# A convolution regrouped by row parity, and a scan layer's hand-written order written anew (one Trainium2 core)

## The chip, the core and the metric

The kernel runs on one core of one Trainium2 chip. The metric is device microseconds of that core. Before the change it takes 26001.39 us, the median of three runs from 25991.08 to 26007.60 us.

## The reference, cut to what matters

The input is 8 images of 128 x 128 positions and 96 channels. Layer 0 (a Fourier filter and a feed-forward net) is untouched by the change. Layer 1 sees the same numbers as 4 images of 32 x 256, and does:

```python
xz = x @ W_in.T;  xc, z = xz[..., :192], xz[..., 192:]
xc = silu(depthwise_conv3x3(xc, conv_w) + conv_b)      # 9 taps a channel
u = stack([xc, xc[reversed]])                          # two directions
dt_r, B, C = split(u @ x_proj);  delta = softplus(dt_r @ dt_proj + b)
# for each direction, channel and state n of 16, along the whole image:
h = exp(delta * A_n) * h + (delta * u) * B_n
y = sum_n(h * C_n);  y = y_forward + y_backward + u * D
out = (y * silu(z)) @ W_out.T                          # then residual, FFN
```

In the code a row of the convolution is 128 positions; a chunk has 8 rows, 1024 positions.

## The kernel before

The trace shows layer 0 for about 4956 us, then the scan layer (`scan_layer`) to the end. Its work goes in **jobs**: batches are taken in four pairs, and for each pair 16 chunks forward (`d == 0`) and then 16 backward (`d == 1`), so 128 jobs. A job has 12 **blocks** (32 channels with 4 states each on the 128 partitions) and a block has 4 **units** `j` (four of the 16 states each), so 48 units. In a block:

- TensorE spreads `delta * u` over the states into the PSUM tile `dub` (L1268, one buffer; two products of 512 columns, each recorded as two matmuls).
- ScalarE makes the decays `da = exp(delta * A)` (L1281), one per unit, in PSUM, two buffers.
- VectorE makes the **injections** `hp = bt * dub` (L1298): one instruction for units 0 and 1 and one for units 2 and 3, 2048 wide. Then it runs the **scan** of each unit over `hp` (L1333).
- GpSimd multiplies each scanned unit by `ct` (L1349, tile `hc`, three buffers), and TensorE sums over the states into `y` (L1358, `total`).
- ScalarE saves the scan's last column (L1342, `keep`).

In a **shared** block ScalarE copies `dub` to SBUF (`fetch`, L1310, tile `dus`), GpSimd does the injection of unit 3 (L1317) and VectorE's second injection is only 1024 wide. `SHARE` names 10 of 12 blocks forward and 4 of 12 backward.

Beside the scans, a forward job does the convolution for the forward job two places later (18 places earlier work for the next pair's first chunks): per job three tiles, each in two halves of nine diagonal products (L1101, tile `pv`), an eviction with bias on ScalarE (L1115), a silu between two table loads (L1126, L1127), and a store to `ud`. Each job also prepares the next one's `delta` and `du` (`prepare_steps`: L1162, L1179, L1190, softplus between two table loads L1193 and L1194, L1201). Backward jobs also gate, project, normalise and run the feed-forward net (`finish_steps`).

The order is written by hand. `plan(at, f)` notes a step with a time in units (48 a job, `UN`), and `emit` records all steps sorted by that time; each engine then works off its own queue strictly in that order. SyncE issues every DMA, in that order too. So a number in `plan` is a place in queues, not a time. In a block that begins at `gb`, the VectorE order before is: injection 0 (`gb`), scan 0, injection 2 (`gb + 1`), scans 1, 2, 3. The other tiles that matter: `hp` has four buffers of two units, `bt` three, `ct` five, `dlb` (the delta broadcast, by DMA L1255) three, `y` one PSUM bank, and `pp` one bank for all small products.

Of the kernel before, what the change touches and what calls it, by code (L numbers as in the profile page):

```python
# [29 lines left out]
TC = 1024  # L30
# [10 lines left out]

def col(ap, p0=None, p1=None):

    v = ap.rearrange("(p o) -> p o", o=1)
    return v if p0 is None else v[p0:p1]
# [8 lines left out]
class Plan:  # L54
# [17 lines left out]
    def emit(self):  # L72
        for _, _, f in sorted(self.steps, key=lambda x: x[:2]):
            f()
# [887 lines left out]
def scan_layer(tc, p, x2d, xcd, zsd, ud, yfd, dld, bcd, out):  # L962
# [11 lines left out]
    with ExitStack() as ctx:  # L974
# [13 lines left out]
        cwt = cp.tile([128, 2, 9], F32, name="cwt")  # L988
        cbt = cp.tile([128, 2], F32, name="cbt")
        for k, parts in enumerate(kinds):  # L990
            for q, c in parts:
                nc.sync.dma_start(cwt[q, k, :], p.conv_w[c, :])
                nc.sync.dma_start(cbt[q, k : k + 1], col(p.conv_b, c.start, c.stop))
        cdiag = cp.tile([128, 2, 9, 128], F32, name="cdiag")
        for k in range(2):
            for j in range(9):
                nc.vector.tensor_scalar(
                    cdiag[:, k, j, :], ident, cwt[:, k, j : j + 1], None, ALU.mult
                )
# [74 lines left out]
        def conv_steps(plan, bp, c, slots):  # L1074
# [3 lines left out]

            def load(t, st):
                def f():  # L1080
                    xin = wk.tile([128, HB + 2, W + 2], F32, tag="xin", name="xin")
                    nc.gpsimd.memset(xin[:, :, 0:1], 0.0)
                    nc.gpsimd.memset(xin[:, :, W + 1 : W + 2], 0.0)
                    for q, b, ch in tile_parts(0, t):
                        nc.sync.dma_start(
                            xin[q, :, 1 : W + 1],
                            xcd[ds(bp * 2 + b, 1), ch, c * HB : c * HB + HB + 2, :].rearrange(
                                "o d h w -> (o d) h w"
                            ),
                        )  # L1090
                    st["xin"] = xin

                return f

            def taps(t, st, i, js):
                def f():
                    if js[0] == 0:
                        st["pv"] = ps1.tile([128, HB // 2, W], F32, tag="pp", name="pv")
                    for j in js:
                        r = i * (HB // 2) + j // 3  # L1100
                        nc.tensor.matmul(  # L1101
                            st["pv"],
                            cdiag[:, kind(t), j, :],
                            st["xin"][:, r : r + HB // 2, j % 3 : j % 3 + W],
                            start=(j == 0),
                            stop=(j == 8),
                        )

                return f

            def evict(t, st, i, hs):
                def f():
                    if i == 0:
                        st["pre"] = w1.tile([128, TC], F32, tag="pre", name="pre")
                    nc.scalar.activation(  # L1115
                        st["pre"][:, hs],
                        st["pv"].rearrange("p h w -> p (h w)"),
                        AF.Identity,
                        bias=cbt[:, kind(t) : kind(t) + 1],
                    )  # L1120

                return f
# [8 lines left out]
            def store(t, st):  # L1131
                def f():
                    nc.sync.dma_start(ud[bp % 2, t, :, c * TC : (c + 1) * TC], st["pre"])

                return f

            for t, begin in enumerate(slots):
                st = {}
                plan(begin[0] - 9, load(t, st))
                for at, (i, hs) in zip(begin, halves()):  # L1140
                    for n, js in enumerate(((0, 1), (2, 3), (4, 5), (6, 7), (8,))):
                        plan(at + n, taps(t, st, i, js))
                    plan(at + 4.4, evict(t, st, i, hs))
                plan(begin[1] + 5, silu(t, st))
                plan(begin[1] + 6.9, store(t, st))

        def prepare_steps(plan, bp, d, c, k, at0):


            k.u, k.du = [None] * 3, [None] * 3  # L1150
# [5 lines left out]
            def project(i, hs):  # L1156
                def f():
# [7 lines left out]
                    k.px = px  # L1165
# [3 lines left out]
            def projected(hs):  # L1169
                nc.scalar.copy(k.bc[:, hs], k.px)  # L1170
# [5 lines left out]
            def delta(t, st, i, hs):  # L1176
                def f():
# [4 lines left out]
                    st["pd"] = pd  # L1182
# [3 lines left out]
            def biased(t, st, i, hs):  # L1186
# [3 lines left out]
                nc.scalar.activation(st["w"][:, hs], st["pd"], AF.Identity, bias=bias)  # L1190
# [12 lines left out]
            for t, at in ((0, 0.4), (1, 3.2), (2, 4.2)):  # L1203
                plan(at0 + at, lambda t=t: load(t))
            for i, hs in halves():
                plan(at0 + 9.2 + 1.3 * i, project(i, hs))
                plan(at0 + 10.2 + 1.1 * i, lambda hs=hs: projected(hs))
            plan(at0 + 12, store_bc)
            for t, at in ((0, PREP[0]), (2, PREP[1]), (1, PREP[2])):
                st = {}  # L1210
                for i, hs in halves():
                    plan(at0 + at["delta"][i], delta(t, st, i, hs))
                    plan(
                        at0 + at["delta"][i] + 0.6,
                        lambda t=t, st=st, i=i, hs=hs: biased(t, st, i, hs),
                    )
                plan(at0 + at["softplus"], lambda st=st: softplus(st))
                plan(at0 + at["mul"], lambda t=t, st=st: mul(t, st))
                plan(at0 + at["store"], lambda t=t, st=st: store(t, st))

        def scan_steps(plan, bp, d, c, k, at0, share):

            bt, ct = {}, {}
# [67 lines left out]
            def inject(blk, j, units):  # L1293
                def f():
                    shared = "dus" in blk and j == 2
# [18 lines left out]
            def inject_shared(blk, units):  # L1314
                def f():
                    hp = blk["hp"] = states_of(blk, 2, units)
                    nc.gpsimd.tensor_tensor(  # L1317
                        hp[:, 1, :], bt[blk["b2"], 2][:, 1, :], blk["dus"], ALU.mult
                    )
# [106 lines left out]
            for m, (b2, t, rr) in enumerate(pairs):  # L1426
# [3 lines left out]
                if m % 3 == 0:  # L1430
                    plan(gm - 12.5, load_b(b2, 0))
                    plan(gm - 3.5, load_b(b2, 2))
                    for j, ahead in enumerate((11.5, 2.5, 1.5, 0.5)):
                        plan(gm - ahead, load_c(b2, j))
                plan(gm - 5, load_pair(pr))
                plan(gm + 2.4, load_z(pr))
                plan(gm + 1.95, open_pair(pr))
                for k2 in range(2):
# [3 lines left out]
                    plan(gb - 7, load_delta(blk))  # L1442
                    plan(gb - 2.5, spread(blk))
                    units = [{} for _ in range(NG)]
                    if 2 * m + k2 in share:
                        plan(gb + 0.1, fetch(blk))
                        plan(gb + 0.5, inject_shared(blk, units))
                    for j, un in enumerate(units):
                        g = gb + j
                        plan(g - 1, decay(blk, j, un))  # L1450
                        plan(g + 1 - 0.05, keep(un))
                        plan(g + 1, read(blk, j, un))
                        plan(g + 2, total(blk, j, un, pr))
                    for at1, f, j in (
                        (0.00, inject, 0),
                        (0.01, scan, 0),
                        (1.00, inject, 2),
# [5 lines left out]
                plan(gm + 9.6, close_pair(pr))  # L1463
                plan(at0 + GATE[m], gate(pr))
                plan(gm + 13.5, store_pair(pr))
            return prs

        def finish_steps(plan, bp, c, prs, i, at0, x2_at, at):
# [181 lines left out]
        PREP = tuple(  # L1650
            {"delta": (a0, a1), "softplus": e, "store": e + 1.9, "mul": m}
            for a0, a1, e, m in (
                (12.2, 13.2, 16.2, 19.3),
                (24.2, 25.2, 28.2, 31.3),
                (37.2, 38.2, 41.2, 45.3),
            )
        )

        SLOTS = ((3.2, 16.2), (26.2, 31.1), (39.1, 43.6))

        def conv_slots(bp, n):
# [3 lines left out]
            if bp > 0 and n < 2:  # L1665
                ahead = [18] * 3
            elif bp > 0 and n == 2:
                ahead = [18, 18, 2]
                slots = ((3.2, 14.3), (19.0, 30.1), SLOTS[2])
# [4 lines left out]
        SHARE = ((0, 1, 2, 3, 4, 6, 7, 8, 9, 11), (1, 4, 7, 10))  # L1674
        GATE = (9.9, 17.9, 25.9, 37.3, 41.9, 50.5)

        FINISH = (
            (
                (14.5, (28.2, 29.6, 30.2, 31.2, 32.2, 40.2, 42.2, 42.2, 44.2, 44.8, 45.4, 46.2,
                46.4, 47.2, 46.6, 47.2, 47.4, 48.2, 47.6, 48.2, 48.4, 48.6, 49.2, 50.2, 52.2,  # L1680
                53.2)),
                (27.5, (40.2, 43.2, 43.8, 44.4, 45.2, 46.2, 49.2, 50.2, 51.2, 51.8, 54.2, 54.8,
                55.2, 55.4, 55.2, 56.2, 56.4, 56.6, 63.2, 63.8, 64.2, 65.2, 70.6, 71.4, 73.2,
                76.2)),
            ),
            (
                (43.5, (52.2, 54.2, 54.8, 55.2, 56.3, 57.2, 60.2, 61.2, 62.2, 62.8, 66.2, 66.8,
                68.2, 69.2, 68.2, 69.2, 69.4, 70.2, 69.6, 70.2, 71.2, 71.4, 74.2, 75.2, 77.2,
                78.2)),
                (55.5, (64.2, 65.6, 66.2, 68.2, 68.2, 76.2, 77.2, 77.2, 78.2, 78.8, 79.4, 80.2,  # L1690
                80.4, 80.6, 80.6, 81.2, 81.4, 82.2, 81.6, 82.2, 82.4, 83.2, 83.8, 84.6, 85.2,
                89.4)),
            ),
        )
        with tc.manual_schedule():
# [4 lines left out]
            for bp in range(B // 2):  # L1700
# [4 lines left out]
                for n, (d, c) in enumerate(jobs):  # L1705
# [3 lines left out]
                    share = SHARE[0 if d == 0 and (bp == 0 or n > 0) else 1]  # L1709
# [10 lines left out]
            plan.emit()  # L1720
# [126 lines left out]
```

## Time and profile before

| | us |
|---|---|
| median of three runs | 26001.39 |
| the profiled execution | 25993.76 |
| its span, first to last instruction | 25992.0 |
| busy in the span: PE / DVE / ACT / POOL | 22274.3 / 24026.8 / 17774.3 / 21599.5 |
| DMA, share of the 16 engines | 42.3% |

The engines are PE (TensorE), DVE (VectorE), ACT (ScalarE), POOL (GpSimd), SP (SyncE); PEld is the weight load. A line of the group view gives source line, engine, operation, what it writes and reads, its shape and count, and then busy time, mean of one in ns, and idle time before it. The view of waits says who waited for whom: total us, times, longest. The view of stretches gives, for a window, each engine's busy us with its instruction count, then the granted TensorE clock as a share, the DMA share and GB/s. In the time line a bracket tells how long the engine sat idle before the instruction and what released it. SPq is SyncE's DMA queue.

### The profile page before, as it was taken

How to read it: one execution, taken by the hardware profiler on the slowest of the kernel's cores; microseconds unless marked ns; L12 is line 12 of the kernel's file. 1: busy time of each engine (PE TensorE's matmuls, PEld its weight loads, DVE VectorE, ACT ScalarE, POOL GpSimd, SP SyncE). 2: the span in 40 equal slices, each digit the busy share in tenths (PEclk: the TensorE clock that was granted, in tenths of full speed). 3: DMA queues.
4: the chain of work that ended last, by engine and by line, in shares of the span. 5: the costliest groups of instructions: out<-in, count | busy, mean ns of one | idle time of the engine just before them, and what ended most of it. 6: DMA issues, size and time to landing. Idle time of an engine off the chain costs nothing.

```text
span 25992.0 us, 271847 instructions
## 1 busy us (share of the span) xinstructions
PE 22274.3 (86%) x85072; PEld 8926.1 (34%) x85072; DVE 24026.8 (92%) x18135; ACT 17774.3 (68%) x31518; POOL 21599.5 (83%) x13561
## 2 busy tenths in 40 slices
PE   8999999888997777888977778888777788887777
PEld 7777777522222222222222222222222222222222
DVE  7888888699999999999999999999999999999998
ACT  6887777566667777666677776666777766657776
POOL 5666666488889999888899998888999988889998
PEclk9999999999998888999988889999888899988888
DMA  3333333344444444444444444444444444444443
GB/s 89 95 94 91 92 89 88 110 152 150 151 152 142 142 142 140 152 152 152 153 142 141 141 140 152 152 152 153 142 141 141 141 151 153 153 144 140 141 142 117
DMA packets 1887419, 3513.54 MB, mean 135 GB/s; under 512 B 564702, under 2 KB 999510, under 8 KB 1885946
## 3 DMA queue, kind: packets, MB, share of 16 engines
q1 hardware_dynamic: 1885972, 3496.15, 42.3%
q8 instruction: 676, 11.08, 0.2%
q14 instruction: 771, 6.32, 0.1%
HBM read 2739.33 MB, written 756.17 MB: 134 GB/s over the span
## 4 chain that ended last, share of the span: by engine, by line
DVE 31%; PE 21%; issue 10%; ACT 10%; POOL 9%; DMA 0%; DVEq 0%; POOLq 0%; SPq 0%; ACTq 0%
DVE hp L1333 19%; DVE hp L1298 12%; PE pv L1101 7%; PE y L1358 6%; POOL hc L1349 6%; PE dub L1268 4%; ACT da L1281 2%; PE y L1400 1%; ACT L1194 1%; ACT L1193 1%; ACT dus L1310 1%; PE pd L1179 1%; PE px L1162 1%; ACT w L1193 1%; POOL hp L1317 1%
## 5 line engine op out<-in xcount | busy, mean ns | idle before, releaser
L1349 POOL TENSOR_TENSOR hc<-hp,ct 128x1024 f32<-128x1024 f32 x6144 | 14376.0, 2359 | 1280.2 <-DVE hp L1333 1035.2
L1333 DVE TENSOR_TENSOR_SCAN hp<-da,h,hp 128x1024 f32<-128x1024 f32 x6144 | 14169.7, 2338 | 662.6 <-ACT da L1281 494.6
L1358 PE MATMUL y<-hc,sely 128*32 128x512 f32 x24576 | 7157.9, 671 | 2284.0 <-POOL hc L1349 2270.9
L1281 ACT ACTIVATE da<-dlb,at 128x1024 f32<-128x1024 f32 x6144 | 6847.6, 1115 | 0.3 <-ACT h L1342 0.3
L1298 DVE TENSOR_TENSOR hp<-bt,dub 128x2048 f32<-128x2048 f32 (+1 forms) x3072 | 6015.8, 1958 | 430.1 <-ACT dus L1310 273.2
L1268 PE MATMUL dub<-du,selx 128*128 128x512 f32 x6144 | 3484.5, 695 | 485.7 <-DVE hp L1298 485.3
L1101 PE MATMUL pv<-xin,cdiag 128*128 128x512 f32 x6912 | 3511.9, 627 | 75.7 <-ACT pre L1115 54.9
L1342 ACT COPY h<-hp 128x1 f32<-128x1 f32 x6144 | 1152.2, 188 | 3296.7 <-DVE hp L1333 3280.3
L1358 PEld LDWEIGHTS y<-hc,sely 128*32 128x32 f32 x24576 | 964.5, 113 | 6824.9 <-POOL hc L1349 4973.6
L1317 POOL TENSOR_TENSOR hp<-bt,dus 128x1024 f32<-128x1024 f32 x878 | 2075.0, 2363 | 788.8 <-ACT dus L1310 781.3
L1268 PEld LDWEIGHTS dub<-du,selx 128*128 128x128 f32 x6144 | 1224.6, 215 | 2581.6 <-issue 1355.4
L1101 PEld LDWEIGHTS pv<-xin,cdiag 128*128 128x128 f32 x6912 | 1181.3, 192 | 2462.3 <-issue 2061.5
L1115 ACT ACTIVATE pre<-pv,cbt 128x512 f32<-128x512 f32 x384 | 263.9, 687 | 1589.5 <-PE pv L1101 1447.7
L1310 ACT COPY dus<-dub 128x1024 f32<-128x1024 f32 x878 | 887.5, 1011 | 471.8 <-DVE hp L1298 471.7
L110 POOL TENSOR_SCALAR ln_v<-ln_v 128x4 f32<-128x4 f32 x768 | 199.6, 260 | 1125.5 <-DVE ln_v L106 1105.4
L1179 PE MATMUL pd<-bc,dtw 12*128 12x512 f32 x1536 | 977.4, 719 | 9.9 <-ACT w L1190 7.5
L1201 POOL TENSOR_TENSOR du<-w,u 128x1024 f32<-128x1024 f32 x384 | 906.6, 2361 | 42.5 <-ACT w L1193 42.5
L111 POOL TENSOR_TENSOR ln_r<-ln_v,mhalf 128x4 f32<-128x4 f32 x768 | 888.4, 1157 | 64.0
L790 PE MATMUL ring<-xnt,win 96*128 96x512 f32 x1536 | 801.2, 630 | 70.1 <-ACT xnt L784 69.0
L1162 PE MATMUL px<-u,xpw 128*76 128x512 f32 x1536 | 756.4, 630 | 2.2 <-ACT bc L1170 1.2
L1582 ACT CAST ff_h<-ph 128x512 f16<-128x512 f32 x768 | 442.1, 576 | 449.0 <-PE ph L1569 449.0
L1190 ACT ACTIVATE w<-pd,dtb 128x512 f32<-128x512 f32 x768 | 523.7, 682 | 298.8 <-PE pd L1179 263.3
(191 smaller groups left out, 31103.0 us busy)
## 6 DMA issues: line engine op xcount, KB each, us to landing
dlb<-dld SPq DMA_DIRECT2D x1536, 512.0 KB, 4.1
bt<-bcd SPq DMA_DIRECT2D x1024, 512.0 KB, 5.3
ct<-bcd SPq DMA_DIRECT2D x1024, 512.0 KB, 3.9
u<-ud SPq DMA_DIRECT2D x384, 512.0 KB, 5.5
dld<-w SPq DMA_DIRECT2D x384, 512.0 KB, 2.9
ud<-pre SPq DMA_DIRECT2D x192, 512.0 KB, 4.3
yf<-ud SPq DMA_DIRECT2D x768, 128.0 KB, 3.8
yfd<-yo SPq DMA_DIRECT2D x384, 256.0 KB, 6.1
```

What stands on the lines that cost most here:

```text
L1101: nc.tensor.matmul(st["pv"], cdiag[:, kind(t), j, :], st["xin"][:, r : r + HB // 2, j % 3 : j % 3 + W], start=(j == 0), stop=(j == 8),)
L1162: nc.tensor.matmul(px, xpw[:, d, t, :], k.u[t][:, hs], start=(t == 0), stop=(t == 2))
L1179: nc.tensor.matmul(pd, dtw[4 * NST : NX, d, t, :], k.bc[4 * NST : NX, hs], start=True, stop=True)
L1268: nc.tensor.matmul(blk["du"][:, hs], selx[:, blk["r"], :], k.du[blk["t"]][:, hs], start=True, stop=True,)
L1281: nc.scalar.activation(un["da"], blk["dl"], AF.Exp, scale=at[:, d, blk["kb"], j : j + 1])
L1298: nc.vector.tensor_tensor(hp[:, 0:n, :], bt[blk["b2"], j][:, 0:n, :], blk["du"].rearrange("p (o t) -> p o t", o=1).to_broadcast([128, n, TC]),
L1310: nc.scalar.copy(blk["dus"], blk["du"])
L1317: nc.gpsimd.tensor_tensor(hp[:, 1, :], bt[blk["b2"], 2][:, 1, :], blk["dus"], ALU.mult)
L1333: nc.vector.tensor_tensor_scan(h, da, h, un["init"], op0=ALU.mult, op1=ALU.add)
L1342: nc.scalar.copy(un["init"], un["h"][:, last : last + 1])
L1349: nc.gpsimd.tensor_tensor(un["hc"], un["h"], ct[blk["b2"], j], ALU.mult)
L1358: nc.tensor.matmul(y[q, :], sely, un["hc"][:, hs], start=False, stop=(j == NG - 1),)
```

## The change

Three things change in the scan layer, and nothing in layer 0.

**Six products for nine.** A convolution tile holds 64 channels twice: partitions 0 to 63 the even rows, 64 to 127 the odd rows. A product's 128 x 128 weight then carries two taps (the diagonal, and one 64 x 64 corner that reaches the other parity), and six products over four row pairs cover the nine taps. The input comes by four DMAs a tile (before: one or two), the result leaves by four (before: one). The weights take 36 VectorE instructions to build (before: 18) and 12 small loads (before: 6).

**Order of a block.** Every offset of `plan` is now taken from a table `PL`. The VectorE order becomes, forward: scan 2 of the block before, injection 0, its scan 3, injection 2, scans 0, 1, 2. Backward: injection 0, scan 3 of the block before, scan 0, injection 2, scans 1, 2. `fetch` stands ahead of injection 0 and right behind the decay of the block before's unit 3; `keep`, `read` and `total` move, as do the loads, stores, softplus, silu and finishing steps.

**Shares.** 0 is no share, 1 as before, 2 gives GpSimd both units 2 and 3 in one 2048-wide instruction, and VectorE none. Forward jobs: six blocks with 1, two with 2 (10 units as before). Backward jobs, and the first forward job of pairs 1 to 3: seven blocks with 1 (before: four).

```diff
+PL = {'share': ((1, 1, 2, 1, 1, 2, 1, 0, 0, 0, 0, 1), (1, 1, 1, 1, 1, 0, 1, 0, 1, 0, 0, 0),
+           (1, 1, 1, 1, 1, 0, 1, 0, 1, 0, 0, 0)),
+ 'dir': ({
...
+          'ld': -4.15,
+          'spread': -2.82,
+          'inj': [-1.385, -0.77],
...
+          'fetch': -1.63,
+          'ishare': -0.89,
+          'close': 10.26,
+          'decay': [-0.7, -0.82, -1.3, -0.75],
+          'keep': [3.4, 2.72, 2.48, 1.42],
+          'read': [1.95, 1.64, 1.05, 2.84],
+          'total': [3.54, 3.32, 3.17, 3.07],
...
+         {
...
+          'spread': -3.01,
+          'inj': [-1.285, 0.83],
...
+          'fetch': -1.81,
+          'ishare': 0.55,
+          'close': 10.14,
+          'decay': [-1.74, -1.18, -1.83, -1.44],
+          'keep': [5.11, 1.54, 1.17, 0.5],
+          'read': [2.39, 1.7, 1.89, 1.68],
+          'total': [3.46, 2.84, 2.51, 2.83],
...
+ 'slots': ((2.59, 14.73, 20.81, 25.93, -0.67), (25.35, 29.44, 33.54, 41.16, 23.49),
+           (39.92, 44.71, 51.05, 53.43, 34.75)),
+ 'tapd': 1.33,
+ 'cev': 3.19,
...
-        for k in range(2):
-            for j in range(9):
+        for n in range(3):
+            for j in range(6):
+                tap = j if j < 3 else j + 3
                 nc.vector.tensor_scalar(
-                    cdiag[:, k, j, :], ident, cwt[:, k, j : j + 1], None, ALU.mult
+                    cdiag[:, n, j, :], ident, cwt[:, n, tap : tap + 1], None, ALU.mult
+                )
+                r, o = (1, 0) if j < 3 else (0, 1)
+                q = slice(64 * r, 64 * r + 64)
+                nc.vector.tensor_scalar(
+                    cdiag[q, n, j, 64 * o : 64 * o + 64],
...
-                    plan(gb - 7, load_delta(blk))
-                    plan(gb - 2.5, spread(blk))
+                    blk["share"] = share[2 * m + k2]
+                    plan(gb + V["ld"], load_delta(blk))
+                    plan(gb + V["spread"], spread(blk))
                     units = [{} for _ in range(NG)]
-                    if 2 * m + k2 in share:
-                        plan(gb + 0.1, fetch(blk))
-                        plan(gb + 0.5, inject_shared(blk, units))
+                    if blk["share"]:
+                        plan(gb + V["fetch"], fetch(blk))
+                        plan(gb + V["ishare"], inject_shared(blk, units))
                     for j, un in enumerate(units):
                         g = gb + j
-                        plan(g - 1, decay(blk, j, un))
-                        plan(g + 1 - 0.05, keep(un))
-                        plan(g + 1, read(blk, j, un))
-                        plan(g + 2, total(blk, j, un, pr))
+                        plan(g + V["decay"][j], decay(blk, j, un))
+                        plan(g + V["keep"][j], keep(un))
+                        plan(g + V["read"][j], read(blk, j, un))
+                        plan(g + V["total"][j], total(blk, j, un, pr))
                     for at1, f, j in (
-                        (0.00, inject, 0),
+                        (V["inj"][0], inject, 0),
                         (0.01, scan, 0),
-                        (1.00, inject, 2),
+                        (V["inj"][1], inject, 2),
                         (1.01, scan, 1),
                         (2.00, scan, 2),
                         (3.00, scan, 3),
                     ):
                         plan(gb + at1, f(blk, j, units))
```

## The prediction

> **What bounds the kernel now.** I read the view of stretches first, cut at job starts (a job is 72 VectorE scans and injections in the time line): ten forward jobs, twelve backward jobs, and the last forward job, which has no convolution beside it.
>
> ```profile
> 5763.00:7401.40 1638.40, 1471.23 (x3844) 408.81 (x3840) 1517.80 (x721) 1002.86 (x1440) 1423.75 (x671) 0.95 0.47 152
> 8052.60:9998.00 1945.40, 1522.37 (x4896) 469.56 (x4896) 1892.49 (x866) 1413.79 (x2629) 1782.52 (x1021) 0.85 0.42 141
> 23193.60:23346.80 153.20, 111.39 (x276) 26.15 (x276) 150.93 (x74) 86.70 (x129) 141.69 (x62) 0.83 0.42 139
> ```
>
> After the length come PE, PEld, DVE, ACT, POOL and the granted clock. A forward job takes 163.8 us with VectorE busy 151.8; a backward job 162.1, VectorE busy 157.7. VectorE bounds both, but forward it stands still 12 us a job. GpSimd is next: 142.4 us a forward job, 148.5 a backward one. The job without convolution takes 153.2 with the same VectorE work: the convolution costs a forward job some 10 us without one instruction on VectorE.
>
> How, the view of waits of the same windows shows: three lines of VectorE forward, one of ScalarE forward, then VectorE backward.
>
> ```profile
> DVE hp L1333 <- ACT da L1281: 51.3, 60, 1.6
> DVE hp L1298 <- ACT dus L1310: 46.2, 30, 2.3
> DVE hp L1298 <- PE dub L1268: 11.3, 10, 1.3
> ...
> ACT pre L1115 <- PE pv L1101: 224.9, 50, 6.9
> ```
>
> ```profile
> DVE hp L1333 <- ACT da L1281: 36.2, 54, 1.1
> ```
>
> Forward, VectorE waits 5.1 us a job for decays, 4.6 for `dus` and 1.1 for `dub`, while ScalarE stands 22.5 us a job at the head of its queue for the convolution's product. The time line joins the two: the eviction waits 5.17 us, everything behind it in ScalarE's queue is late, and the injection starts 2.30 late, the moment `dus` is done.
>
> ```profile
> 6051.26 0.69 ACT L1115 ACTIVATE pre<-pv,cbt 128x512 f32<-128x512 f32 x1 [5.17 <-PE pv L1101]
> ...
> 6052.98 1.01 ACT L1310 COPY dus<-dub 128x1024 f32<-128x1024 f32 x1
> ...
> 6054.02 1.22 DVE L1298 TENSOR_TENSOR hp<-bt,dub 128x1024 f32<-128x1024 f32 x1 [2.30 <-ACT dus L1310]
> ```
>
> Prices I take from start to start, in a stretch of VectorE's time line without waits:
>
> ```profile
> 8052.60 2.26 DVE L1298 TENSOR_TENSOR hp<-bt,dub 128x2048 f32<-128x2048 f32 x1
> 8054.97 2.35 DVE L1333 TENSOR_TENSOR_SCAN hp<-da,h,hp 128x1024 f32<-128x1024 f32 x1
> 8057.24 2.26 DVE L1298 TENSOR_TENSOR hp<-bt,dub 128x2048 f32<-128x2048 f32 x1
> 8059.41 6.83 DVE L1333 TENSOR_TENSOR_SCAN hp<-da,h,hp 128x1024 f32<-128x1024 f32 x3
> ...
> 8070.79 1.20 DVE L1298 TENSOR_TENSOR hp<-bt,dub 128x1024 f32<-128x1024 f32 x1
> 8071.90 6.83 DVE L1333 TENSOR_TENSOR_SCAN hp<-da,h,hp 128x1024 f32<-128x1024 f32 x3
> ```
>
> A wide injection costs 2.37 (8052.60 to 8054.97) when the next instruction scans what it wrote, 2.17 (8057.24 to 8059.41) when it does not; a narrow one 1.11; a scan 2.25 to 2.27, I take 2.26. The sums stand up: forward 12 x 2.37 + 2 x 2.17 + 10 x 1.11 + 48 x 2.26 = 152.4, plus waits of 10.9, is 163.3 of 163.8; backward 12 x 2.37 + 8 x 2.17 + 4 x 1.11 + 108.5 = 158.7, plus 3.1, is 161.8 of 162.1.
>
> **The change, part by part.**
>
> Order. Injection 0 is now followed by the neighbour's scan 3, so all are priced 2.17: 12 x 0.20 = 2.4 us less a job, both ways.
>
> Shares. Forward VectorE has 12 + 4 wide and 6 narrow injections: 16 x 2.17 + 6 x 1.11 + 108.5 = 149.9. Backward 17 wide and 7 narrow: 153.2. GpSimd keeps 10 units forward, so 142.4 stays under 149.9. Backward it takes three more; four `hc` in a row take 9.30, so 2.33 each: 148.5 + 7.0 = 155.5, above VectorE's 153.2. Backward the bound moves to GpSimd, and 155.5 is the floor.
>
> Six for nine. The products cost 0.43 us a record at full clock (18 records in 7.96 us): 36 records fewer, 15.5 us of TensorE a forward job. None of that is on VectorE's path; it pays only through ScalarE, whose eviction waits less. Its place moves too: the eviction stands 0.53 units behind the last products (before 0.4), and the sums `y`, on which TensorE waits for GpSimd at its queue's head, stand 3.1 to 3.5 units behind their unit (before 2), so the products are less held up. Bounds: nothing gained (10.9 us of waits stay), or all (0.8, the wait of the job without convolution).
>
> The new wait. `fetch` now precedes injection 0, and both read `dub`; the copy is recorded first, so injection 0 waits for it in 8 blocks forward, 7 backward. It stands behind the decay of unit 3, which needs scan 1 over. From there: 1.11 for the decay, 1.01 for the copy and an estimated 0.1 for starts (the injection above starts 0.03 after its copy's end), 2.2 in all, beside scan 2 of 2.26. It just fits. In blocks 1, 3, 5 and 11 forward the copy of `y` (0.58) stands between: 0.5 late, 2 us a job. Behind the waiting injection stand scan 3 and all VectorE work. Softplus and silu with their loads (2 x 1.28 + 1.06 = 3.6 us) now stand mostly behind `fetch`, beside injection 0, scan 3 and injection 2 (5.5 us), so I give them nothing. With 1 us of other delays, forward waits are 3.1 a job, 153.0 in all; bounds 150.5 and 158. Backward VectorE waits 3.1 now behind the feed-forward's ScalarE work; on GpSimd's 155.5 I put 2.5 for the two engines' uneven steps: 158.0; bounds 155.5 and 162.3, where half of GpSimd's present idle time (162.1 - 148.5 = 13.6) remains.
>
> The spread (`dub`) follows injection 2 and precedes `fetch`. At full clock it took 1.96, at a low clock 3.78:
>
> ```profile
> 6000.48 1.96 PE L1268 MATMUL dub<-du,selx 128*128 128x512 f32 x4 [0.94 <-DVE hp L1298]
> ...
> 6013.96 3.78 PE L1268 MATMUL dub<-du,selx 128*128 128x512 f32 x4
> ```
>
> From injection 2 to the copy's turn there are scans 0 and 1 and a decay, 2 x 2.26 + 1.2 = 5.7 us forward, one scan less backward, 3.5. Forward it is hidden either way; backward at full clock only, and at the low one 0.3 late, hidden by GpSimd. Less work on TensorE makes the low clock likelier: the job without convolution had 0.83 against 0.95, and yet waited least. The Trainium skill, "TensorE: Matmul & The Clock Gate", Part 1, speaks against the change here: after an idle window of about 3.4 us the array's clock falls to half. By that rule with every spread on the path, 12 x 1.8 = 22 us a job would be lost; by the row of the job at 0.83, nothing.
>
> DMAs. A forward job issues 17 more (8 inputs, 9 stores), at 0.33 to 0.61 each under 10 us of SyncE's queue, beside about 60 issues. The load of a block's delta falls from 7 units ahead of its block to 4.15 and 3.25; its first decay stands 0.7 and 1.74 ahead, so 3.45 units (11 us) are left forward and 1.5 (5 us) backward, for a landing of 4.1 (median of `dlb`). That is thin backward only if SyncE issues no earlier than the step's place. It does issue earlier: in the view of its waits the longest line is this load waiting for a buffer to come free.
>
> ```profile
> SPq L1255 <- ACT da L1281: 4090.6, 617, 13.0
> ```
>
> I put the DMAs at nothing, with 1 us a job as the other end. `keep` (0.19) moves from ahead of a decay to behind it: up to 0.2 less between a scan's end and the next decay, counted at nothing.
>
> Before the first scan (4956 to 5110) TensorE does twelve nine-product groups at 8.0 us; at 5.3 that is 32 less, 4 more for six small loads: -28. The 57 us after the last scan stay, plus or minus 6.
>
> **Sum.** 62 forward jobs with convolution: 62 x (153.0 - 163.8) = -670. Two without, 154.4 to 151: -7. Backward 64 x (158.0 - 162.1) = -262. Start -28. Together -967; 25993.8 - 967 = 25027 for an execution like the profiled one; the median of the runs stands 7.6 above it: **25034 us**. All lower bounds give 64 x 149.9 and 64 x 155.5 in place of 10457 and 10368, the scans' own total: about 24,690.
>
> **The rivals.**
>
> - GpSimd's saturation (0.17): backward at 162.3, nothing gained, the rest as forecast: 25,310. For it: 155.5 of 158 leaves no slack and `hp` has four buffers. Against: GpSimd behind by a unit or two never starves.
> - The waits stay (0.12): ScalarE's evictions were not the cause, or others take their place. Forward gains its 2.5 us alone, 161.3: 25,540. Against it stands the job of 153.2.
> - Slower (0.06): `dus` is late ahead of injection 0 everywhere. Its present wait is 1.54 when it comes (46.2/30); at all 15 blocks of a forward and a backward job that is 23 us, against 163.8 + 162.1 - 149.9 - 155.5 = 20.5 gained: 26,160. It decides from 1.4 us a block.
> - The floors are reached (0.05): 24,690.
>
> **How the numbers follow.** The forecast has 0.60, its own range 24,740 to 25,300. With GpSimd's rival and most of the second, 24,740 to 25,480 holds 8 in 10. A measurement of this kernel tells about 0.2%, 52 us. Faster by more: the forecast, the floors and the first two rivals without a small remainder, 0.92; within it 0.02; slower 0.06.
>
> **What would show it.** Right: forward jobs near 153 with "pre <- pv" waits under 10 us a job; VectorE's waits for `dus` moved to the wide injection; GpSimd busy 155 of 158 backward; the clock forward below 0.95. Wrong: VectorE waiting over 1.4 us a block for `dus`, GpSimd waiting for `y` or for scans backward, or waits for a DMA on VectorE or ScalarE.

## The result, and the profile after

The changed kernel takes 26051.34 us, the median of 13 runs (26038.47 to 26066.16), beside 25992.88 for the kernel before (13 runs, 25982.32 to 26007.60). The ratio is 1.0022, with a 95% interval of 1.0014 to 1.0031: 0.2% slower, where 25034 us and a range of 24740 to 25480 were predicted. The profiled execution took 26050.59 us, its span 26048.8.

The view of stretches of the kernel after, ten forward jobs and twelve backward ones (length, then PE, PEld, DVE, ACT, POOL with counts, clock, DMA share, GB/s):

```profile
5765.80:7388.80 1623.00, 1338.01 (x3480) 362.25 (x3480) 1501.96 (x701) 984.04 (x1421) 1417.31 (x648) 0.90 0.50 153
8040.10:10009.10 1969.00, 1476.90 (x4896) 483.03 (x4896) 1843.68 (x866) 1442.78 (x2664) 1863.75 (x1057) 0.88 0.42 140
```

A forward job takes 162.3 us (163.8 before; 153.0 forecast), a backward job 164.1 (162.1; 158.0 forecast). Yet VectorE is busy 150.2 and 153.6 us a job, and GpSimd 155.3 backward: the three floors were forecast at 149.9, 153.2 and 155.5. So the work shrank as foretold, and waiting ate it: VectorE now stands still 12.1 us of a forward job and 10.5 of a backward one.

The view of waits in the same two windows, VectorE's main lines and two of ScalarE forward, then VectorE's backward (total us, times, longest):

```profile
DVE hp L1405 <- ACT dus L1417: 109.1, 50, 3.6
DVE hp L1405 <- issue: 11.1, 8, 1.4
...
ACT yo L1522 <- PE y L1473: 47.1, 28, 2.6
ACT pre L1208 <- PE pv L1193: 24.7, 22, 2.1
```

```profile
DVE hp L1405 <- ACT dus L1417: 91.9, 46, 4.9
DVE hp L1405 <- POOL ff_y L1734: 15.1, 10, 1.5
```

Of three kinds of wait forward one is left, and at 12.1 us a job it is larger than the three were together (10.9). ScalarE's wait for the convolution's product fell from 22.5 to 2.5 us a job, and VectorE's wait for decays has nearly gone (12.6 us in the whole scan layer, 492.6 before). But injection 0 waits for the copy `dus`, by the view 10.9 us a job forward and 7.7 backward. The lines that name `issue` or GpSimd in front of injection 0 are the copy too: in every shared block where it is late, it starts 0.03 to 0.10 us after the copy's end (in one case 0.44). Where nothing waits, injection 0 starts 2.24 us after the scan ahead of it. Against that, and as the mean of the ten forward jobs, it is late by 0 / 0.45 / 0 / 3.65 / 3.13 / 1.56 / 2.53 us in blocks 0 to 6, by 1.28 in block 11, and by 0 in the unshared blocks 7 to 10: 12.6 in all.

Why, the time line of ScalarE shows at block 4 of a forward job (start, duration, what; the bracket is idle time before it), and VectorE's beside it:

```profile
11692.85 1.12 ACT L1386 ACTIVATE da<-dlb,at 128x1024 f32<-128x1024 f32 x1 [1.57 <-DVE hp L1448]
11693.91 0.67 ACT L1294 ACTIVATE w<-pd,dtb 128x512 f32<-128x512 f32 x1
11694.59 1.28 ACT L1297 ACT_TABLE_LOAD   x1
11695.89 1.06 ACT L1297 ACTIVATE w<-w 128x1024 f32<-128x1024 f32 x1
11696.96 1.28 ACT L1298 ACT_TABLE_LOAD   x1
11698.26 1.12 ACT L1386 ACTIVATE da<-dlb,at 128x1024 f32<-128x1024 f32 x1
11699.31 1.00 ACT L1417 COPY dus<-dub 128x1024 f32<-128x1024 f32 x1
```

```profile
11690.48 6.82 DVE L1448 TENSOR_TENSOR_SCAN hp<-da,h,hp 128x1024 f32<-128x1024 f32 x3
11700.35 2.29 DVE L1405 TENSOR_TENSOR hp<-bt,dub 128x2048 f32<-128x2048 f32 x1 [3.05 <-ACT dus L1417]
```

Scan 1 is over at 11690.48 + 2 x 2.26 = 11695.0, and decay 3 could start then. It starts at 11698.26, because softplus and its two table loads stand ahead of it in the queue. The copy follows the decay, and the injection starts 0.04 after the copy's end. In block 6 it is silu with its loads; in blocks 1, 3, 5 and 11 the copy of `y` or an eviction, with what each waits for itself.

Block 9 is the control. There, too, silu and its loads stand ahead of decay 3, but the block has no copy, and injection 0 starts without a wait (end of the burst on ScalarE, then VectorE):

```profile
6043.48 1.28 ACT L1220 ACT_TABLE_LOAD   x1
6044.78 1.12 ACT L1386 ACTIVATE da<-dlb,at 128x1024 f32<-128x1024 f32 x1
```

```profile
6037.61 6.82 DVE L1448 TENSOR_TENSOR_SCAN hp<-da,h,hp 128x1024 f32<-128x1024 f32 x3
6044.35 2.26 DVE L1405 TENSOR_TENSOR hp<-bt,dub 128x2048 f32<-128x2048 f32 x1
```

In the run e4 below, where blocks 7 and 9 are shared, injection 0 is late by 5.90 and 3.01 us in them.

### The profile page after: what moved, and what is told of

The parts are those of the page before. It is cut to its first block, busy times and chain, and to the rows that moved or that the text cites. A ratio compares the mean times of both kernels' runs of the same rounds, so it can differ in the third digit from the quotient of the medians.

```text
span 26048.8 us, 268368 instructions
## 1 busy us (share of the span) xinstructions
PE 21191.9 (81%) x82768; PEld 8705.7 (33%) x82768; DVE 23661.7 (91%) x18031; ACT 17822.4 (68%) x31597; POOL 22017.7 (85%) x13640
## 4 chain that ended last, share of the span: by engine, by line
DVE 36%; issue 18%; PE 12%; POOL 9%; ACT 7%; DMA 1%; SPq 0%; POOLq 0%; DVEq 0%; ACTq 0%
DVE hp L1448 19%; DVE hp L1405 17%; POOL hc L1464 7%; PE dub L1373 4%; PE y L1473 3%; ACT da L1386 2%; ACT dus L1417 2%; PE po L1608 1%; PE pv L1193 1%; ACT L1298 1%; POOL du L1305 0%; PE y L1515 0%; POOL hp L1432 0%; ACT yo L1522 0%; PE px L1266 0%
## 5 line engine op out<-in xcount | busy, mean ns | idle before, releaser
L1448 DVE TENSOR_TENSOR_SCAN hp<-da,h,hp 128x1024 f32<-128x1024 f32 x6144 | 14067.3, 2332 | 12.6 <-ACT da L1386 12.6
L1473 PE MATMUL y<-hc,sely 128*32 128x512 f32 x24576 | 6794.9, 658 | 1022.8 <-POOL hc L1464 1013.4
L1405 DVE TENSOR_TENSOR hp<-bt,dub 128x2048 f32<-128x2048 f32 (+1 forms) x2950 | 5797.1, 1965 | 1502.7 <-ACT dus L1417 1176.9
L1373 PE MATMUL dub<-du,selx 128*128 128x512 f32 x6144 | 3832.0, 756 | 1661.6 <-DVE hp L1405 1327.1
L1193 PE MATMUL pv<-xin,cdiag 128*128 128x512 f32 x4608 | 2332.1, 630 | 152.9 <-ACT pre L1208 93.6
L1457 ACT COPY h<-hp 128x1 f32<-128x1 f32 x6144 | 944.3, 185 | 1042.1 <-DVE hp L1448 1037.4
L1193 PEld LDWEIGHTS pv<-xin,cdiag 128*128 128x128 f32 x4608 | 852.6, 199 | 1675.4 <-issue 1444.2
L1515 PE MATMUL y<-yf,ddiag 128*128 128x512 f32 x768 | 532.1, 781 | 484.5 <-ACT yo L1522 484.5
L1522 ACT COPY yo<-y 128x512 f32<-128x512 f32 x768 | 446.0, 581 | 631.4 <-PE y L1473 631.2
L1608 PE MATMUL po<-wo,yo 128*128 128x194 f32 x3072 | 622.5, 353 | 195.0 <-POOL yo L1529 195.0
```

The costliest lines, as they stand in the source:

```text
L1193: nc.tensor.matmul(st["pv", i], cdiag[:, groups(t)[i][1] // 64, j, :], st["xin"][:, i, r : r + HB // 2, j % 3 : j % 3 + W], start=(j == 0) ...
L1373: nc.tensor.matmul(blk["du"][:, hs], selx[:, blk["r"], :], k.du[blk["t"]][:, hs], start=True, stop=True,)
L1405: nc.vector.tensor_tensor(hp[:, 0:n, :], bt[blk["b2"], j][:, 0:n, :], blk["du"].rearrange("p (o t) -> p o t", o=1).to_broadcast([128, n, TC]),
L1448: nc.vector.tensor_tensor_scan(h, da, h, un["init"], op0=ALU.mult, op1=ALU.add)
L1457: nc.scalar.copy(un["init"], un["h"][:, last : last + 1])
L1473: nc.tensor.matmul(y[q, :], sely, un["hc"][:, hs], start=False, stop=(j == NG - 1),)
```

## The experiments

All times are medians, and each ratio is to the kernel before, run beside it on the same chip, with its 95% interval. In the short diffs the first place of a kind is the forward one, the second the backward one. My theory after the result: the copy ahead of injection 0 makes VectorE wait for whatever ScalarE has in its queue. The rivals: the low clock makes the spreads late; GpSimd is the bound backward; the six products themselves cost something. Four of the twelve expected times held (e2, e8, e9, e12); e3 came out faster than its range, and the other seven slower.

**e1, the copy ahead of decay 3.**

```diff
-          'fetch': -1.63,
+          'fetch': -2.8,
...
-          'fetch': -1.81,
+          'fetch': -3.0,
```

> The changed kernel with the copy of dub (fetch) moved up in ScalarE's queue, from behind the decay of the block before's unit 3 to ahead of it (forward -1.63 to -2.8, backward -1.81 to -3.0); nothing else. Theory A (ScalarE's queue): injection 0 waits for the copy only because decay 3, copies of y, evictions, biases and table loads stand ahead of it; the waits fall from about 12 us a forward and 10 us a backward job to under 4, forward jobs near 153, backward near 157: 25,050 us, at most 25,300. Theory B (TensorE's spread ends too late, at the low clock): dub is no earlier, so the waits stay, 25,950 or more.

25832.39 us, 0.9939 [0.9924, 0.9954]. VectorE's waits in the whole scan layer:

```profile
DVE hp L1448 <- ACT da L1386: 598.0, 365, 3.2
DVE hp L1405 <- ACT dus L1417: 258.5, 181, 3.8
```

The waits for `dus` fell from 1165.5 to 258.5, but scans now wait 598.0 for decays that stand behind the copy. A forward job falls to 158.2, a backward one rises to 165.2. The chain was the right one; that it would end there was wrong.

**e2, no shares.** Without a share there is no copy.

```diff
+PL = {'share': ((0,) * 12, (0,) * 12, (0,) * 12),
```

> The changed kernel with no shared block: no copy of dub, VectorE does all injections 2048 wide. Theory A: no wait ahead of injection 0 is left; 24 x 2.17 + 48 x 2.26 = 160.6 us of VectorE a job, about 161 with small waits, 128 jobs: 25,780 us (25,700 to 25,900), so faster than the changed kernel although VectorE has 957 units more to inject. Theory B: the spread is late for unshared blocks as well, 10 us of waits a job stay, 171 a job: 27,000.

25707.61 us, 0.9889 [0.9874, 0.9904]. These are all of VectorE's waits in the scan layer:

```profile
DVE hp L1404 <- PE dub L1372: 15.8, 17, 1.5
DVE hp L1447 <- ACT da L1385: 2.1, 4, 0.6
```

VectorE has 24 wide injections a job here, 24 x 2.17 + 108.5 = 160.6 us, and jobs take 160.4 and 160.6: nothing is waited for at clocks of 0.89 and 0.87. That speaks against the clock rival; the kernel's own trace settles it, in the paragraph on the clock below. The 957 in the expectation counts shared blocks; VectorE gets back 61 x 10 + 67 x 7 = 1079 units. In this order, taking work from VectorE through these shares cost more than the shares were worth.

**e3, the six products alone**, in the order and shares of before. The eviction keeps its place in the order, so it now stands 2.4 units behind the last of three groups of products.

```diff
-for n, js in enumerate(((0, 1), (2, 3), (4, 5), (6, 7), (8,))):
+for n, js in enumerate(((0, 1), (2, 3), (4, 5))):
```

> The kernel before with six products in place of nine, all places in the queues and all shares as before. Theory A: ScalarE's waits for the convolution's product fall from 22.5 us a forward job to about 10, and VectorE's waits from 10.9 to about 5: forward jobs 158, backward unchanged, start 28 less: 25,600 us (25,450 to 25,800). Rival (the evictions' wait was no cause, or more DMAs cost what is gained): forward jobs 163 to 164, 25,950 or more.

25398.51 us, 0.977 [0.9754, 0.9786]. The forward jobs, and the same two waits as above:

```profile
5729.80:7266.40 1536.60, 1315.75 (x3480) 356.85 (x3480) 1512.78 (x721) 1009.07 (x1441) 1421.58 (x671) 0.93 0.53 162
```

```profile
DVE hp L1360 <- ACT da L1308: 11.1, 41, 1.6
...
ACT pre L1132 <- PE pv L1117: 1.5, 4, 0.4
```

A forward job takes 153.7 us with VectorE busy 151.3; backward nothing changes. This is under the expected range: VectorE's waits fell from 10.9 to 1.1 us a job, where 5 was expected. The products are worth 598 us by themselves; what of it is fewer products and what the eviction's greater distance from them, no run tells apart.

**e4, the new order with the old shares.**

```diff
-PL = {'share': ((1, 1, 2, 1, 1, 2, 1, 0, 0, 0, 0, 1), (1, 1, 1, 1, 1, 0, 1, 0, 1, 0, 0, 0),
+PL = {'share': ((1, 1, 1, 1, 1, 0, 1, 1, 1, 1, 0, 1), (0, 1, 0, 0, 1, 0, 0, 1, 0, 0, 1, 0),
```

> The changed kernel with the shares of the kernel before (ten of twelve forward, four of twelve backward). Theory A: the wait goes with shared blocks that have ScalarE work ahead of the copy. Forward 150.0 of VectorE's own work plus 12 to 15 of waits, about 164; backward 156.3 plus about 5, about 161.5: 26,000 us (25,900 to 26,100). Theory B: backward 156.3 plus 10, 166: 26,300.

26215.65 us, 1.0085 [1.007, 1.01]; forward 167.3 with VectorE idle for 16.8 (13.1 of it noted as waiting for `dus`), backward 162.4. With e3 the three parts follow, added one after the other: six products 25398.51 - 25996.64 (the kernel before, beside e3) = -598, new order 26215.65 - 25398.51 = +817, new shares 26051.34 - 26215.65 = -164.

**e5, the copy behind injection 0.**

```diff
-          'fetch': -1.63,
+          'fetch': -1.3,
...
-          'fetch': -1.81,
+          'fetch': -1.2,
```

> The changed kernel with the copy of dub recorded just behind injection 0 (forward -1.63 to -1.3, backward -1.81 to -1.2) in place of ahead of it; nothing else. Theory A (the copy is recorded ahead of injection 0, and both read dub, so injection 0 inherits every delay of ScalarE's queue): injection 0 no longer waits for ScalarE; the copy has scan 3 of the block before to hide under. Forward 150 plus about 2, backward 156 to 158 with GpSimd near 155: 25,000 us (24,850 to 25,200). Rival (ScalarE has too little time in shared blocks wherever the copy stands): the waits reappear before injection 2 and before scans, 7 us or more a job in both directions, 25,700 or more.

25661.88 us, 0.987 [0.9855, 0.9884]; 160.2 us a job both ways, no better than without shares (e2). VectorE's main waits in the scan layer, and one of ScalarE's:

```profile
DVE hp L1448 <- ACT da L1386: 668.8, 338, 3.9
DVE hp L1405 <- PE dub L1373: 294.2, 190, 3.6
...
ACT dus L1417 <- DVE hp L1405: 895.7, 466, 3.6
```

No injection 0 waits for `dus` any more, but now the copy waits for injection 0, at the head of ScalarE's queue; a burst of softplus or silu then comes late, and the next decay behind it (2.56 us in block 1, 3.09 in block 11). As in e1, the lateness moved to the scans, and the time is close to the rival's 25,700.

**e6, six products and seven shares backward, old order.**

```diff
-        SHARE = ((0, 1, 2, 3, 4, 6, 7, 8, 9, 11), (1, 4, 7, 10))
+        SHARE = ((0, 1, 2, 3, 4, 6, 7, 8, 9, 11), (0, 1, 3, 4, 6, 7, 10))
```

> The kernel before with six products and with seven shared blocks backward (0, 1, 3, 4, 6, 7, 10) in place of four; all places in the queues as before. Theory: VectorE backward loses 3 x 1.06 = 3.2 us a job, GpSimd gains 7.0 to 155.5: backward 162.1 to 159.5, forward 153.7: 25,230 us (25,150 to 25,400). Rival (GpSimd near its limit gives the gain back): 25,400 or more.

25473.09 us, 0.9797 [0.9781, 0.9814]. A backward job rises from 162.1 to 163.9 though VectorE's work falls to 154.7: waits for decays of 5.8 and for `dus` of 2.0 a job. These seven shares backward do not pay in the old order either.

**e7, VectorE's new order alone**: the two injections at their new places, the copy just behind injection 0 (not ahead of it, as in the changed kernel) and GpSimd's shared injection moved along; all else as in e3.

```diff
-                        (0.00, inject, 0),
+                        ((-1.385, -1.285)[d], inject, 0),
...
-                        (1.00, inject, 2),
+                        ((-0.77, 0.83)[d], inject, 2),
```

> The kernel before with six products and VectorE's new order (injection 0 ahead of the neighbour's scan 3, injection 2 at its new place), the copy of dub right behind injection 0, all shares and all other places as before. Theory: injection 0 at 2.17 in place of 2.37, 12 x 0.2 = 2.4 us less a job both ways; forward 151.5, backward 160: 25,110 us (25,000 to 25,300). Rival (the new order itself breaks the cover of decays and spreads): slower than the 25,400 of six products alone.

26908.42 us, 1.0352 [1.0336, 1.0367]: 1800 us above the theory's number. In ten forward jobs, VectorE's first wait and one of TensorE's:

```profile
PE y L1385 <- POOL hc L1376: 331.2, 143, 5.0
...
DVE hp L1325 <- PE dub L1295: 184.9, 77, 6.2
```

Injection 0 moved up by 1.4 units and the spread that feeds it did not. The spread stands behind sums `y` that wait for GpSimd at the head of TensorE's queue, so injection 0 waits 18.5 us a job for `dub`. An order is a set: one engine's part of it costs 1500 us against e3.

**e8, shares only where the copy comes in time.**

```diff
+PL = {'share': ((1, 1, 2, 0, 0, 2, 0, 0, 0, 0, 0, 0), (0, 0, 1, 0, 1, 0, 0, 0, 0, 0, 0, 0),
```

> The changed kernel with shares only where its trace shows the copy of dub in time or nearly (forward blocks 0 and 1 with 1, blocks 2 and 5 with 2; backward blocks 2 and 4); nothing else. Theory A: VectorE gets 6 injections back forward (1.06 each, 149.9 to 154.1 with the two-wide ones unchanged) and 5 backward (153.2 to 158.5), and the waits of the blocks taken out go (forward 10.7 of 12.6, backward 9.9 of 10.9): 156 forward, 159.5 backward, 25,370 us (25,250 to 25,500). Rival (lateness of ScalarE only moves on to decays): forward 162 or more, 25,700.

25494.9 us, 0.9812 [0.9795, 0.9828]: 157.0 forward, 160.5 backward, with 38.8 us of waiting for `dus` left in the whole scan layer. Four shared blocks forward and two backward, in place of eight and seven, gain 26051.34 - 25494.9 = 556 us.

**e9, the old forward order and the new backward one without shares**, six products. The forward half of `PL` and the convolution's places are those of before, and so are the shares of forward jobs.

```diff
+PL = {'share': ((1, 1, 1, 1, 1, 0, 1, 1, 1, 1, 0, 1), (0,) * 12, (0, 1, 0, 0, 1, 0, 0, 1, 0, 0, 1, 0)),
...
+          'inj': [0.0, 1.0],
...
+          'fetch': 0.1,
```

> Six products; forward jobs with every place and share of the kernel before, backward jobs with the changed kernel's places and no share. Theory: forward as in the run with six products alone, 153.7; backward as in the run without shares, 160.6, against 162.1: 25,290 us (25,200 to 25,380), the fastest so far. Rival (the two orders disturb each other at the 7 changes of direction, or the finishing steps' places need the shares): 25,400 or more.

25354.75 us, 0.9756 [0.9742, 0.9771]: 153.5 and 160.4 a job.

**e10, the copy of `y` behind the copy of `dub`.**

```diff
-          'close': 10.26,
+          'close': 10.45,
...
-          'close': 10.14,
+          'close': 10.25,
```

> The changed kernel with the copy of y moved from just ahead of the copy of dub to just behind it (forward 10.26 to 10.45, backward 10.14 to 10.25); nothing else. Theory A: in the blocks where it stood between, forward 1, 3, 5 and 11 and backward 1 and 3, the wait before injection 0 falls by the copy and by its own wait for TensorE: about 5 us a forward job (of 12.6) and 4 a backward job (of 10.9): 25,480 us (25,350 to 25,750). Theory B (the spread is late) or a queue that is late anyway: 26,000.

25815.56 us, 0.9935 [0.992, 0.995]; forward 159.1. Blocks 1, 5 and 11 no longer wait and block 3 is late by 0.53 in place of 3.65, but block 2 by 1.08 in place of 0 and block 4 by 4.22 in place of 3.13.

**e11, also the first tile's softplus, silu and second half of the convolution behind it** (and one bias), and no shares backward.

```diff
-          'prep': [[10.01, 12.9, 13.91, 20.94, 14.79],
+          'prep': [[10.1, 12.9, 14.45, 20.94, 14.79],
...
- 'slots': ((2.59, 14.73, 20.81, 25.93, -0.67),
+ 'slots': ((2.59, 15.25, 22.45, 25.93, -0.67),
```

> As the run with the copy of y behind, and forward the three other steps that stand ahead of a copy of dub moved behind it (softplus of the first tile 13.91 to 14.45, its first bias by 0.09, the convolution's first tile: second half 14.73 to 15.25, silu 20.81 to 22.45); backward no shares. Theory A: forward all waits before injection 0 go, 152 to 153; backward 160.6 as in the run without shares: 25,180 us (25,080 to 25,400). Rival (ScalarE's steps now make the decays late): forward 157 or more, 25,500.

25593.14 us, 0.9849 [0.9834, 0.9864]; forward 159.0, no better than e10. VectorE waits 2.9 us a job for decays, 2.9 for `dus`, 1.9 for GpSimd's injections and 1.1 for `dub`: the lateness moved to other steps.

**e12, the best of both halves**: e9 with five shared blocks backward, and there the copy behind injection 0.

```diff
-PL = {'share': ((1, 1, 1, 1, 1, 0, 1, 1, 1, 1, 0, 1), (0,) * 12,
+PL = {'share': ((1, 1, 1, 1, 1, 0, 1, 1, 1, 1, 0, 1), (1, 0, 0, 1, 1, 0, 1, 0, 1, 0, 0, 0),
...
-          'fetch': -1.81,
+          'fetch': -1.2,
```

> Six products; forward jobs with every place and share of the kernel before; backward jobs with the changed kernel's places, five shared blocks (0, 3, 4, 6, 8) and the copy of dub recorded just behind injection 0. Theory A: forward 153.5; backward VectorE 160.4 - 5 x 1.06 = 155.1 plus about 3 of waits for decays and dub, 158: 25,210 us (25,100 to 25,360), faster than 25,355. Rival (a share's copy always costs ScalarE as much as it saves VectorE): backward 160.5, 25,360.

25260.4 us, 0.9716 [0.97, 0.9732], the fastest version found. Its two stretches and its longest wait in the scan layer:

```profile
5723.40:7259.90 1536.50, 1315.71 (x3480) 356.89 (x3480) 1512.78 (x720) 1008.83 (x1440) 1421.33 (x671) 0.93 0.54 162
7881.10:9798.40 1917.30, 1449.97 (x4896) 475.00 (x4896) 1866.41 (x866) 1422.73 (x2641) 1807.59 (x1033) 0.90 0.44 143
```

```profile
DVE hp L1447 <- ACT da L1385: 239.6, 399, 2.7
```

Forward is e3's (153.7). Backward VectorE is busy 155.5 of 159.8, the best backward job of all runs, with GpSimd at 150.6.

## Why the prediction was wrong

**The step that failed** is the new wait's price: "Softplus and silu with their loads … now stand mostly behind `fetch` … so I give them nothing", with "2 us a job" for the copy of `y` and "1 us of other delays". Together that was 3.1 us of forward waiting; 12.1 came. By block, blocks 4 and 6 are late by 5.7 us behind a burst that was given nothing, and blocks 1, 3, 5 and 11 by 6.9 where 2 were put. Softplus stands at 13.91 in the order and decay 3 of block 3 at 12 + 3 - 0.75 = 14.25: that burst comes ahead of decay and copy, and so does silu's in block 6 (3.13 and 2.53 us late). The word "mostly" hid these two of a job's six bursts; both meet shared blocks. In block 3 the copy of `y`, priced by its own 0.58, first waits 2.6 us for TensorE's `y` at the head of ScalarE's queue, and the bias activation follows it (3.65). In block 5 the eviction waits up to 2.14 for its product (1.56). In block 1 nothing is waited for, and the forecast's 0.5 holds (0.45). Where nothing stands between, as in blocks 0 and 2, the forecast's chain holds: the copy ends 2.18 us after the decay may start, beside 2.24 to the injection.

**Backward**, 2.5 us of unevenness were put on GpSimd's 155.5. The copy had no term there. GpSimd was busy 155.3, but the job took 164.1, 8.8 more: injection 0 is late in all seven shared blocks, by 0.25 to 3.02 us, 11.0 in all. So the "slower" rival had the mechanism: 12.6 + 11.0 = 23.6 us over 15 shared blocks is 1.6 us a block, above its 1.4. It was given 0.06 on "its present wait is 1.54", a mean over the few blocks in which a wait shows. Its time, 26,160, was not met. It took GpSimd's 155.5 for the backward floor; from VectorE's 153.2 the break-even is 163.8 + 162.1 - 149.9 - 153.2 = 22.8 us, 1.5 a block, and VectorE stood idle for 12.1 + 10.5 = 22.6. Hence a time near that of before. Nor is the copy late "everywhere": forward, blocks 0 and 2 have no wait.

**The other steps.** VectorE's floors were right to 0.4 us, and e2 shows the price of 2.17 again. The gain of the six products was right in kind, and e3 shows it almost whole: ScalarE's wait for `pv` is 2.5 us a job, under the 10 named, and e3 has the forward job at 153.7 with no new order at all. That this meets the forecast's 153.0 is luck, since the forecast reached it with the new order's gain and the copy's price in it. The products themselves fell from 549.6 to 364.9 us in ten jobs, 18.5 a job (15.5 forecast). GpSimd as a bound backward did not decide. In the kernel after, GpSimd itself waits, 40.7 us in twelve jobs for scans, and each late injection follows the copy; e2 gives it less work and still takes 160.6, VectorE's own sum. The start gained nothing: the first scan came at 5115.1, against 5112.6 before (-28 forecast), though the products take less time there. Of the chain that ended last between 4955 and 5118 us they made up 48.5% before and 20.8% after; after, SyncE's issues of weights, inputs and stores (L1125, L1177, L1231) make up 20.0%, where none had over 0.7% before. The tail fell from 57.5 to 51.5 us.

**The sum**, span to span, over all jobs of the trace: forward, 62 jobs, -76 us (-670 forecast), backward, 64 jobs, +134 (-262), the two jobs without convolution 157.2 + 154.8 - 155.7 - 153.2 = +3 (-7), start +2 (-28), tail -6: +57, the measured 56.8. Ten jobs from the middle show the forward gain larger, 62 x (162.3 - 163.8) = -93, because jobs at a change of direction do worse: the first forward job of pairs 1 to 3 takes 164.9 to 166.0 us, 161.7 to 162.1 before.

**The clock.** Forward it fell from 0.95 to 0.90, as foreseen. The Trainium skill, "TensorE: Matmul & The Clock Gate", Part 1, says an array idle for a window of some 3.4 us drops to half its clock. In this trace spreads do take 3.78 us at times. Yet in unshared blocks behind such a spread injection 0 starts at most 0.16 us late, and in shared backward blocks it is no later behind a spread of over 3.3 us than behind one of under 2.2 (1.46 and 1.56 on average; forward 1.91 and 1.49). The copy hardly waits for the spread, in the whole scan layer:

```profile
ACT dus L1417 <- PE dub L1373: 18.5, 62, 1.2
```

The measurement decides: here the slower clock has next to no price on the path.

**Where the gain went.** The six products gave 598 us. The new order saves 0.20 a block on VectorE and puts ScalarE's copy on the path ahead of injection 0, and lost 817; without copies (e2) it has no waits to speak of. The new shares leave out blocks 7 and 9, late by 8.9 us together in e4, and returned 164. Moving the copy (e1, e5) or the bursts (e10, e11) shifts the lateness to decays or GpSimd: within this order no run got a shared forward job under 157.0, while the old order has it at 153.5. That no other arrangement of it could do so isn't shown.

## What to carry to other kernels

When a step moves ahead of the bounding engine's next instruction, write down the queue of the engine that does the step, in order, with every wait in it; an operation that waits at the head of that queue costs its wait on top of its duration (in block 3 a copy of 0.58 us waits 2.6 first). The wait between two readers of one tile came here from the order in which they are recorded, so look at which of them stands first. Take a change of several parts apart first: here one part gave 2.3%, and the others took it back.

## What the runs showed of the hardware

- Injection 0 and the copy both only read `dub`, and yet the one recorded second starts when the first is over: the injection 0.04 us after the copy's end in the time line above, the copy at the earliest 0.03 after the injection's end in e5. In none of the 878 shared blocks of the kernel before, nor of the 957 of the kernel after or of e5, do the copy and an injection of the same block overlap. The profile reads the wait from a semaphore, so the program orders them; what would happen without it was not tried.
- A pair of table loads around a 1024-wide activation holds ScalarE's queue for 1.28 + 1.06 + 1.28 = 3.6 us; in e3 all six a job cost VectorE no more than 1.1 us, in the kernel after the two ahead of blocks 4 and 6 cost 5.7. The burst is as dear as the slack at its place. The Trainium skill, "ScalarE: Activation LUTs", What ACT_TABLE_LOAD costs, puts a switch at some 2.66 us, a load of 1283 ns and a drain. The load is the same here, but in the time line above the next activation starts 1.30 us after the load's start, so no drain shows.
- Part of what TensorE saved in the convolution went into its other work while the granted clock fell from 0.95 to 0.90: the products fell by 18.5 us a forward job, and the other lines rose by 3.3 together, 1.6 of it the spreads (248.9 to 264.8 us in ten jobs).
